# Layers 0 and 1 of a four-layer graph network: seven half products, both layers of a batch in turn, queues in program order

## The chip, the core and the metric

One core of a Trainium2 chip runs the whole kernel. The time is device microseconds of one execution; the median of three runs is compared. The engines are TensorE (PE, with its weight loads PEld), VectorE (DVE), ScalarE (ACT), GpSimd (POOL) and SyncE (SP), which here only issues DMAs.

## The reference

Sixteen graphs (batches) of 1024 nodes with 256 features, everything in float32, `adj` a dense 1024x1024 matrix per batch. Every layer is `x = x + layer(relu(layernorm(x)), adj)`:

```python
# layer 0: attention whose logits are e_n + f_m; e_n cancels in the quotient
h = hidden @ W_w.T + W_b
u = adj * exp(e[:, :, None] + f[:, None, :] + a_b);  a = u / sum(u, axis=2)
layer0 = a @ h
# layer 1: degree-normalised convolution
d = (sum(adj, -1) + 1e-5) ** -0.5
layer1 = (d[:, :, None] * adj * d[:, None, :]) @ (x @ weight) + bias
# layer 2: gated units over the nodes one after the other (a scan over 1024 nodes)
# layer 3: neighbour sums, then two products with an RMS norm between
```

So layers 0 and 1 each need, per batch, one sum over neighbours (`adj` times a 1024x256 matrix), a small product with a 256x256 matrix, and the weighted row sums of `adj`. Layer 2 visits the nodes in an order that is worked out on the chip from the zeros of `adj`.

## The kernel before

`layers_0_1` runs first, then `layer_2`, then `layer_3`. Only `layers_0_1` and the generator `orders` that runs inside it are touched by the change.

**A batch in layers 0 and 1.** `adjT` of a batch is loaded as two halves `at` of 512 columns (2 MB each), which stay for both layers; there are five such buffers. `prepare` takes the layer norm's statistics (L276, L277 on DVE, the power -0.5 in L83 on POOL), makes `q` and the attention weights `g`. `layer_0` computes the two weighted row sums (`pd`, L347, then `pn`, L357), then the sums over neighbours: `sums` has four parts, one for each half of the columns and each half of the 256 features, of eight 128x128 by 128x512 matmuls each (L295), copied from PSUM by ACT (L298) and DVE (L300). Then eight tiles are multiplied with `w0` (L365) and added to `x` by DVE (L366). `reshape` takes the statistics of the new `x` and ACT writes the normed `h1` (L287); `layer_1` does the same with `h1` and `w1` (L396, L397).

**The order of batches.** In step i, `layer_0(i)` comes first and `layer_1(i - 1)` after it, so that the norm between the two layers of a batch has products of another batch beside it. The parts of other work (`prepare`, `reshape`, jobs) are put between the four parts of the sums. No order is written out by hand: the framework's scheduler sets each engine's order, so that DVE's small instructions of several tasks are mixed.

**The order of the nodes.** `orders` returns two generators, which are advanced at such places. `places` reads diagonal blocks of `adj` in pieces of 16 rows (eight loads of 128 KB each, L99, prepared by L100) and assigns 128 nodes per block to sub-blocks: five small DVE instructions per node (L121 to L126), then ranks (L135, L137). `rest`, from step 9 on, makes index tables (L148, L163, L167), then the longest chains: two DVE instructions per node (L181, L182) on pieces loaded again, then maxima (L187 to L201), PE transposes (L208) and counters (L214 to L222), which become `more`, the register values that layer 2's loops read.

**The jobs.** `put_in_order(b)` is run from step 9 on, two batches a step: it loads diagonal blocks and rows (`ad`, `ab`, L409 to L413, and `h2`, L416), masks and scales them on POOL (L421 to L426), transposes `h2` and `ad` with the permutation `to` (L434, L447, L449) through `pt` in PSUM into the tile `hT`, multiplies `ab` with `h2` (L462), and stores the results for layer 2 with DMAs from POOL. The store of `hT` must end before the tile is written again.

**The start of layer 2** loads weights, `he` and `base`, POOL copies `hs` (L726), PE computes the gates' inputs (L735) and DVE adds the bias (L740).

## Time and profile before

| | |
|---|---|
| median of 3 runs | 4622.65 us (4618.07 to 4628.17) |
| span of the profiled execution | 4622.5 us, the only time that the page gives for it |
| mean granted TensorE clock | 0.978 |
| PE, DVE, POOL, ACT busy | 94%, 55%, 35%, 28% of the span |
| layers 0 and 1 on PE | to 1498.4 us |
| first PE, first DVE instruction of layer 2's gates (L735, L740) | 1511.25, 1520.0 us |

A group's line has the source line, the engine, the operation, the tile written and those read, the shapes, the count, then the busy time in us, the mean of one in ns, and the idle time of the engine before such instructions with what ended it. A float32 matmul shows as two records on PE, so 32 matmuls are "x64"; a transpose shows as one.

### The profile page before, as it was taken

The page shows a single profiled execution, that of the slowest core. Times are in us where ns is not written, and L with a number is a line of the kernel's source. Part 1 is how long each engine was busy: PE and PEld are TensorE (multiplying, and loading weights), DVE is VectorE, ACT ScalarE, POOL GpSimd, SP SyncE. Part 2 cuts the span into 40 slices and gives each one's busy share as a digit, 9 for nine tenths or more (in the row PEclk, how much of TensorE's full clock was granted, in tenths as well). Part 3 has the DMA queues.
Part 4 walks back from the last instruction along what each step waited for, and adds up shares of the span by engine and source line. Part 5 has one row for each costly group of instructions (what it writes and reads, how often), then busy time and mean ns, then how long its engine had stood idle before and what let it go on. Part 6 is the DMA issues. An engine that isn't in the chain of part 4 may idle for free. (4 is left out here: it accounts for less than half of the span.)

```text
span 4622.5 us, 54868 instructions
## 1 busy us (share of the span) xinstructions
PE 4336.9 (94%) x19223; PEld 2956.2 (64%) x19223; DVE 2535.5 (55%) x6436; ACT 1279.5 (28%) x2741; POOL 1623.5 (35%) x1914
## 2 busy tenths in 40 slices
PE   8999799999997899999999999999799999999998
PEld 4444345555554687778787878787655656565656
DVE  6667944555554344444444444445356666676765
ACT  1111111221121232323232323233234333333333
POOL 3222333433333333332332323234244444445352
PEclk9999899999998999999999999999899999999999
DMA  4333244455544644454444454542142222232310
GB/s 150 112 116 100 73 112 146 164 194 188 156 145 154 196 138 154 131 166 141 154 121 151 131 159 135 167 144 73 55 142 89 100 92 92 88 104 82 110 46 19
DMA packets 530989, 576.78 MB, mean 125 GB/s; under 512 B 42544, under 2 KB 439472, under 8 KB 528304
## 3 DMA queue, kind: packets, MB, share of 16 engines
q1 hardware_dynamic: 499536, 460.27, 32.0%
q0 software_dynamic: 31040, 111.44, 6.9%
q8 instruction: 206, 3.38, 0.3%
q14 instruction: 207, 1.70, 0.1%
HBM read 469.65 MB, written 116.65 MB: 127 GB/s over the span
## 5 line engine op out<-in xcount | busy, mean ns | idle before, releaser
L295 PE MATMUL pa<-at,h 128*128 128x512 f32 x1088 | 495.3, 608 | 33.0 <-DVE ag L300 33.0
L295 PE MATMUL pa<-at,q 128*128 128x512 f32 x960 | 423.6, 594 | 0.0
L623 PE MATMUL pf<-hb,ab 128*128 128x256 f32 x1568 | 407.9, 383 | 14.5 <-DMA hb<-hs_d 5.7
L295 PEld LDWEIGHTS pa<-at,h 128*128 128x128 f32 x1088 | 209.7, 196 | 277.6 <-issue 231.5
L735 PE MATMUL pf<-hs,wx 128*128 128x256 f32 x1536 | 348.9, 381 | 19.2 <-POOL hs L726 17.6
L735 PEld LDWEIGHTS pf<-hs,wx 128*128 128x128 f32 x1536 | 290.6, 191 | 62.5 <-POOL hs L726 19.4
L623 PEld LDWEIGHTS pf<-hb,ab 128*128 128x128 f32 x1568 | 280.3, 191 | 67.2 <-issue 14.2
L295 PEld LDWEIGHTS pa<-at,q 128*128 128x128 f32 x960 | 178.2, 190 | 215.9 <-issue 212.8
L1189 PE MATMUL ph<-bxt,hb 128*128 128x512 f32 x704 | 310.8, 597 | 3.8 <-ACT hb L1173 3.0
L1218 POOL TENSOR_TENSOR ss<-ss,sq 128x512 f32<-128x512 f32 x224 | 280.7, 1271 | 87.1 <-ACT sq L1216 83.4
L1023 POOL DMA_INDIRECT hs_d<-h,table x128 | 129.6, 1013 | 330.0 <-ACTq L1009 150.8
L1279 PEld LDWEIGHTS po<-w,hh 128*128 128x128 f32 x2048 | 235.9, 193 | 9.5 <-issue 7.2
L1279 PE MATMUL po<-w,hh 128*128 128x128 f32 x2048 | 240.1, 277 | 1.4 <-ACT hh L1262 0.7
L1189 PEld LDWEIGHTS ph<-bxt,hb 128*128 128x128 f32 x704 | 133.2, 192 | 164.7 <-issue 159.8
L740 DVE TENSOR_TENSOR gates<-pf,bias 128x512 f32<-128x512 f32 x128 | 88.3, 691 | 238.6 <-PE pf L735 238.6
L1261 DVE TENSOR_TENSOR hh<-hh,po 128x512 f32<-128x512 f32 x256 | 154.5, 681 | 96.7 <-PE po L1258 96.7
L83 POOL TENSOR_TENSOR rs<-rs_v,mhalf 128x8 f32<-128x8 f32 (+1 forms) x65 | 106.9, 1645 | 255.0 <-DVE rs_v L79 241.5
L771 PE MATMUL pf<-bd,h 128*128 128x384 f32 (+4 forms) x512 | 185.6, 454 | 5.3 <-ACT bs L610 2.8
L1216 ACT ACTIVATE sq<-hh 128x512 f32<-128x512 f32 x224 | 141.1, 630 | 164.3 <-DVE hh L1214 125.6
L830 ACT ACTIVATE r<-pr 128x256 f32<-128x256 f32 (+3 forms) x230 | 68.1, 348 | 403.5 <-PE pr L789 389.5
L1214 DVE SCALAR_TENSOR_TENSOR hh<-ph,b,u 128x512 f32<-128x512 f32 x192 | 144.0, 751 | 64.9 <-PE ph L1210 54.8
L774 DVE TENSOR_TENSOR bxt<-bxt,pf 128x384 f32<-128x384 f32 (+4 forms) x256 | 125.0, 501 | 97.0 <-PE pf L771 95.5
(296 smaller groups left out, 8473.1 us busy)
## 6 DMA issues: line engine op xcount, KB each, us to landing
at<-in_adjT SPq DMA_DIRECT2D x64, 1024.0 KB, 7.1
ab<-in_adj SPq DMA_DIRECT2D x128, 512.0 KB, 4.3
bxt<-in_adjT SPq DMA_DIRECT2D x88, 512.0 KB, 6.7
at<-in_adjT SPq DMA_DIRECT2D x40, 512.0 KB, 6.8
ad<-in_adj SPq DMA_DIRECT2D x128, 128.0 KB, 6.2
x_d<-x POOLq DMA_DIRECT2D x16, 1024.0 KB, 5.1
he_d<-h POOLq DMA_DIRECT2D x16, 1024.0 KB, 8.9
heT_d<-hT POOLq DMA_DIRECT2D x16, 1024.0 KB, 4.2
```

The lines of the kernel that those rows point to most:

```text
L295: nc.tensor.matmul(pa, h[:, mt, c * P : (c + 1) * P], at[n0 // 512][:, mt], start=mt == 0, stop=mt == NT - 1)
L623: nc.tensor.matmul(pb, ab[:, jts[k]], hb[:, jts[k]], start=k == 0, stop=k == len(jts) - 1)
L735: nc.tensor.matmul(pg[:, e], wx[:, c, q * D + e * P : q * D + (e + 1) * P], self.hs[:, c], start=c == 0, stop=c == DC - 1)
L771: nc.tensor.matmul(pf, h[:, g, c * P : (c + 1) * P], bd[:, g, b0 : b0 + n, S : S + far], start=True, stop=True)
L774: return lambda: nc.vector.tensor_add(to, to, pf)
L1023: nc.gpsimd.indirect_dma_start(out=hs_d[t][g][:, :], out_offset=row(1, g, t, s), in_=h[:, g], in_offset=None)
L1189: nc.tensor.matmul(pa, h[b][:, mt, c * P : (c + 1) * P], at[b][n0 // NH][:, mt], start=mt == 0, stop=mt == NT - 1)
L1214: nc.vector.scalar_tensor_tensor(hh[q][:, k], ph, b1[:, k : k + 1], u, op0=ALU.add, op1=ALU.add)
L1216: nc.scalar.activation(sq, hh[q][:, k], AF.Square)
L1218: nc.gpsimd.tensor_tensor(ss[q], ss[q], sq, ALU.add)
L1261: nc.vector.tensor_mul(hh[q][:, k], hh[q][:, k], pr)
L1279: nc.tensor.matmul(po[:, n], left[:, c, n * P : (n + 1) * P], right[:, c], start=onto is None and n == 0 and c == 0, stop=c == HH - 1, ski ...
```

## The change

The sums over neighbours are computed from halves in all three dimensions, with seven products of four matmuls in place of eight (`combos`, `sums`). The left factors are `q` or `h1`, combined by four DVE instructions per layer, two of them in place. The right factors are combinations of the quarters of `adjT` that are made once per batch and used in both layers: `t1` and `t3` by an accumulating DMA from POOL (`plus`), `t2` and `t4` by DVE (`add_halves`). One quarter is loaded twice. Ten quarter buffers (1 MB each) take the place of the five halves.

Both layers of a batch now run in turn in step i; only the product with `w1` and the addition to `x` of batch i - 1 are put off, to stand between layer 0 and layer 1 of batch i. The statistics of `x` for layer 0 and layer 2 move from DVE to ACT (`Moments`); the additions of `W_b` and `bias` on POOL work on two tiles at a time.

`manual_schedule` for all five queues: every engine runs its instructions in the order of the program. Other work is placed by hooks between the products. The two generators of `orders` become one, with a planned cost in us at each `yield`; `side(us)` advances it by about that much. Pieces are four rows (eight loads of 32 KB) in two buffers of their own, the next but one fetched when a piece is done. What is left of the generator at the end of the stage is run there. The jobs, two a step from step 9 on, run as a block after the `w1` product and after layer 1; the last two follow in step 16. Layers 2 and 3 are untouched.

The core of the diff (in the hooks, only the calls that the text speaks of):

```diff
-    def piece(j0, op, value):
-        nz = pool.tile([P, S, P], F32, name="ad")
-        for t in range(NT):
-            nc.sync.dma_start(nz[t * B : (t + 1) * B], a["adj"][:, t * P + j0 : t * P + j0 + S, t * P : (t + 1) * P])
-        nc.vector.tensor_scalar(nz[:, :, j0:], nz[:, :, j0:], 0.0, value, op0=op, op1=ALU.mult)
-        return nz
+    R = 4
+    pieces = deque()
+    def fetch(j0):
+        nz = pool.tile([P, R, P], F32, name="pc", bufs=2)
+        for t in range(NT):
+            nc.sync.dma_start(nz[t * B : (t + 1) * B], a["adj"][:, t * P + j0 : t * P + j0 + R, t * P : (t + 1) * P])
+        pieces.append(nz)
+    def piece(j0, op, value):
+        nz = pieces.popleft()
+        nc.vector.tensor_scalar(nz[:, :, j0:], nz[:, :, j0:], 0.0, value, op0=op, op1=ALU.mult)
+        return nz
...
+        fetch(0)
+        fetch(R)
+        yield 9.0
+        for j0 in range(0, P, R):
+            nz = piece(j0, ALU.is_equal, 2 * TOP)
...
+                if j < j0 + R - 1:
+                    yield 1.0
+            if j0 + 2 * R < P:
+                fetch(j0 + 2 * R)
+            yield 1.2
...
+    yield from places()
+    while not now["rest"]:
+        yield 99.0
+    yield from rest()
+now = {"rest": False}
...
+        ET = mybir.EngineType
+        st.enter_context(tc.manual_schedule(engines={ET.PE, ET.DVE, ET.Activation, ET.Pool, ET.SP}))
...
+        quarters = [big.tile([P, 4, 512], F32, name=f"at{k}") for k in range(10)]
+        Q = {b: {} for b in range(B)}
+        def get(b, name, m, n):
+            Q[b][name] = quarters.pop(0)
+            nc.sync.dma_start(Q[b][name], rows(a["adjT"][b])[:, 4 * m : 4 * m + 4, 512 * n : 512 * n + 512])
+        def drop(b, name):
+            quarters.append(Q[b][name])
+        def plus(b, name, other):
+            nc.gpsimd.dma_start(out=Q[b][name], in_=Q[b][other], accum_op=ALU.add)
...
+            def first(self, tiles):
+                junk = psum.tile([P, 512], F32, name="pt")[:, :D]
+                for t in tiles:
+                    nc.scalar.activation(junk, self.x[:, t], AF.Identity, accum_out=self.sum[:, t : t + 1])
...
-        def sums(at, h, ag):
-            def part(n0, c):
-                pa = psum.tile([P, 512], F32, name="pa")
-                for mt in range(NT):
-                    nc.tensor.matmul(pa, h[:, mt, c * P : (c + 1) * P], at[n0 // 512][:, mt],
-                                     start=mt == 0, stop=mt == NT - 1)
-                if c == 0:
-                    nc.scalar.copy(ag[:, c, n0 : n0 + 512], pa)
-                else:
-                    nc.vector.tensor_copy(ag[:, c, n0 : n0 + 512], pa)
-            return [lambda n0=n0, c=c: part(n0, c) for n0 in (0, 512) for c in range(DC)]
+        def combos(h):
+            a11, a12, a21, a22 = (h[:, m * 4 : m * 4 + 4, c * P : (c + 1) * P] for c in range(DC) for m in range(2))
+            s1, s2 = (big.tile([P, 4, P], F32, name=name) for name in ("s1", "s2"))
+            st = {"11": a11, "12": a12, "22": a22, "s1": s1, "s2": s2, "s3": a21, "s4": a12}
+            def first():
+                nc.vector.tensor_sub(s1, a21, a22)
+                nc.vector.tensor_sub(s2, s1, a11)
+            def second():
+                nc.vector.tensor_sub(a21, a11, a21)
+                nc.vector.tensor_add(a12, a12, s2)
+            return st, first, second
+        def sums(b, st, hooks, done=lambda name: None):
+            ag = big.tile([P, DC, N], F32, name="ag", bufs=2)
+            c11, c12, c21, c22 = (ag[:, c, n : n + 512] for c in range(DC) for n in (0, 512))
+            m = Q[b]
+            def product(left, right, pa, start=True):
+                for k in range(4):
+                    nc.tensor.matmul(pa, st[left][:, k], m[right][:, k], start=start and k == 0, stop=k == 3,
+                                     skip_group_check=True)
+                done(right)
+            bank = lambda: psum.tile([P, 512], F32, name="pa", bufs=4)
+            px = bank()
+            product("11", "b11", px)
+            nc.scalar.copy(c11, px)
+            hooks[0]()
+            py = bank()
+            product("12", "b21", py)
+            nc.vector.tensor_add(c11, c11, py)
+            hooks[1]()
+            product("s2", "t2", px, False)
+            nc.scalar.copy(c12, px)
+            hooks[2]()
+            pz = bank()
+            product("s1", "t1", pz)
+            hooks[3]()
+            product("s3", "t3", px, False)
+            nc.scalar.copy(c21, px)
+            nc.vector.tensor_sub(c22, pz, c21)
+            hooks[4]()
+            pw = bank()
+            product("22", "t4", pw)
+            nc.vector.tensor_add(c21, c21, pw)
+            hooks[5]()
+            product("s4", "b22", pz, False)
+            nc.vector.tensor_sub(c12, pz, c12)
+            hooks[6]()
+            return ag
+        def weights(x, ag, w, scale, then=lambda t: None):
+            for t0 in range(0, NT, 2):
+                po = psum.tile([P, 2, D], F32, name="pmm")
+                for t in (t0, t0 + 1):
+                    for c in range(DC):
+                        nc.tensor.matmul(po[:, t - t0], ag[:, c, t * P : (t + 1) * P], w[:, c],
+                                         start=c == 0, stop=c == DC - 1)
...
+                for t in (t0, t0 + 1):
+                    for c in range(DC):
+                        nc.tensor.matmul(po[:, t - t0], ag[:, c, t * P : (t + 1) * P], w[:, c],
+                                         start=c == 0, stop=c == DC - 1)
+                for t in (t0, t0 + 1):
+                    nc.vector.scalar_tensor_tensor(x[:, t], po[:, t - t0], scale[:, t : t + 1], x[:, t],
+                                                   op0=ALU.mult, op1=ALU.add)
+                    then(t)
...
+        def degrees(b):
+            m = Q[b]
...
+            for n0, (top, low) in ((0, ("b11", "b21")), (512, ("t3", "b22"))):
...
+            def run(self):
+                self.turn()
+                self.first()
+                self.order()
+                self.base()
+        def side(us):
+            left[0] += us
+            while left[0] > 0:
+                cost = next(math, None)
+                if cost is None:
+                    break
+                left[0] -= cost
+            left[0] = min(left[0], 0.0)
...
+        jobs = {i: (2 * (i - 9), 2 * (i - 9) + 1) for i in range(9, 16)}
+        jobs[16] = (14, 15)
...
+            def a1():
+                second()
+                add_halves(i, "t4", "t2", "b21")
+                late_norm(hi)
...
+                side(3.0)
+            def a3():
+                side(4.0)
...
+            def a4():
+                nonlocal_["rc"], nonlocal_["deg"] = over(i, ds)
...
+                side(1.5)
...
+                inverse(i, nonlocal_["deg"])
+                if run_a:
+                    run_a.scale()
+                side(2.0)
...
+                side(3.0)
...
+                    for name, mh, nh in (("b11", 0, 0), ("t1", 0, 1), ("b22", 1, 1)):
+                        get(i + 1, name, mh, nh)
+                ag = sums(i, left_of, [a0, a1, a2_, a3, a4, a5, a6])
+                mv = small.tile([P, NT, 2], F32, name="mv")
+                weights(x[i], ag, w0, nonlocal_["rc"], lambda t: stats(x[i], (t,), mv))
...
+                normed(h1[i], x[i], shift, rd, all_)
...
+                weights(x[i - 1], ags[i - 1], w1, dis[i - 1],
...
+                left_of, first, second = combos(h1[i])
+                first()
+                side(2.0)
+            if run_a:
+                run_a.run()
+                run_b.load()
...
+            def d0():
+                if ahead:
+                    plus(i + 1, "t1", "b11")
+                    get(i + 1, "t3", 0, 1)
+                plus_row(x[i], "bias")
+                if m2:
+                    m2.first(all_)
+            def d1():
+                second1()
+                if ahead:
+                    get(i + 1, "b21", 1, 0)
+                    begin_f(i + 1, all_)
+                if m2:
+                    m2.middle()
+                side(2.0)
...
+                    add_f(i + 1, hi)
+                    end_f(i + 1)
+                side(1.0)
...
+            def d5():
+                if ahead:
+                    Q[i + 1]["t2"] = quarters.pop(0)
+                    add_halves(i + 1, "t2", "t1", "b22")
...
+            ags[i] = sums(i, left_of, [d0, d1, d2, d3, d4, d5, d6], lambda name: drop(i, name))
+            if ahead:
+                ds = degrees(i + 1)
+                left_of, first, second = combos(q[i + 1])
+                first()
+                plus(i + 1, "t3", "b22")
+                plus_row(x[i + 1], "W_b")
+                Q[i + 1]["t4"] = quarters.pop(0)
+            if run_b:
+                run_b.run()
+            side(4.0)
+        for _ in math:
+            pass
```

## The prediction, made before the changed kernel ran

> **What bounds the kernel now.** I read the page's busy times first, then busy time by stretch, the groups and waits of the stretch in which layers 0 and 1 run, then the timeline of its ends.
>
> The page; then busy time by stretch (columns: stretch, length, then PE, PEld, DVE, ACT, POOL busy, granted clock, DMA share, GB/s):
> ```profile
> PE 4336.9 (94%) x19223; PEld 2956.2 (64%) x19223; DVE 2535.5 (55%) x6436; ACT 1279.5 (28%) x2741; POOL 1623.5 (35%) x1914
> ```
> ```profile
> 66.65:789.46 722.81, 662.76 (x2068) 340.03 (x2066) 477.37 (x1802) 129.48 (x268) 206.71 (x203) 0.96 0.34 103
> 789.46:1355.05 565.59, 534.13 (x1967) 302.68 (x1965) 302.21 (x905) 118.48 (x240) 213.00 (x228) 0.99 0.54 176
> 1355.05:1498.40 143.35, 120.05 (x437) 73.95 (x435) 67.65 (x257) 24.03 (x46) 47.16 (x48) 0.89 0.39 128
> ```
> PE is the bound: 92% busy in the first stretch (batches before the jobs that put rows in order), 94% in the second (two jobs a batch). DMA is at half or less, ACT at a fifth. The degree products start at 53.08, 94.22 ... 789.46 ... 1355.05: 81.8 us a batch over the first nine, 94.3 over the six with jobs.
>
> The groups (busy, mean ns, then idle before):
> ```profile
> L295 PE MATMUL pa<-at,h 128*128 128x512 f32 x1088 | 495.3, 608 | 33.0 <-DVE ag L300 33.0
> L295 PE MATMUL pa<-at,q 128*128 128x512 f32 x960 | 423.6, 594 | 0.0
> L83 POOL TENSOR_TENSOR rs<-rs_v,mhalf 128x8 f32<-128x8 f32 x48 | 80.1, 1668 | 126.7 <-DVE rs_v L79 113.3 <-DVE mv L277 12.3
> L181 DVE SCALAR_TENSOR_TENSOR ad<-o_sub,ad 128x127 f32<-128x127 f32 (+63 forms) x127 | 37.6, 301 | 0.2
> L182 DVE SCALAR_TENSOR_TENSOR o_bins<-ad,o_bins 128x127 f32<-128x127 f32 (+63 forms) x127 | 37.1, 292 | 0.2
> ```
> The neighbour sums are 919 us of PE. L181/L182 are the chain rows that the old order hid under them.
>
> The PE timeline (start, length, bracket: idle before it):
> ```profile
> 66.65 27.73 PE L295 MATMUL pa<-at,h 128*128 128x512 f32 x64
> 127.39 9.79 PE L295 MATMUL pa<-at,h 128*128 128x512 f32 x16 [3.71 <-DVE ag L300]
> 918.32 7.13 PE L295 MATMUL pa<-at,h 128*128 128x512 f32 x16 [2.25 <-DVE ag L300]
> 1010.11 8.76 PE L295 MATMUL pa<-at,h 128*128 128x512 f32 x16 [2.27 <-DVE ag L300]
> ...
> 1497.94 0.44 PE L468 MATMUL pt<-to,bo 128*128 128x128 f32 x2 [0.57 <-ACT bo L464]
> 1511.25 1.22 PE L735 MATMUL pf<-hs,wx 128*128 128x256 f32 x2 [12.87 <-POOL hs L726]
> ```
> 64 records are 32 matmuls, so one costs 0.866 us. Sixteen records should take 6.93; after waits of 3.71, 2.25 and 2.27 they take 9.79, 7.13 and 8.76. A gap costs itself and up to 2.9 more. Layers 0 and 1 end at 1498.4, and 12.87 of wait follows.
>
> **Products removed.** 28 matmuls for 32, in 2 layers of 16 batches: 128 x 0.866 = 110.8 us off PE. PE work of a batch becomes 2 x 24.2 (sums) + 1.8 (L357) + 2 x 7.0 (L365, L396) + 3.6 (L347) = 67.8 us; a job adds 8.5 (its transposes and L462).
>
> **Cover removed.** Before, layer 1 of the previous batch (28 us) lay between layer 0 of a batch and its own layer 1. Now only the 7.0 us of w1 products do. I count from the start of layer 0's products.
>
> A batch in which `places` runs beside: the seven products and L357 end at 26.1. DVE, from 7.1 on (second product), has evictions 4 x 0.69, combinations 2 x 0.69, t4 2 x 1.38, small rows 1.7 and 10.5 planned units of `side`. One node of `places` is planned at 1.0-1.2, but its five rows (253+165+250+206+308 ns) in strict order, with 0.04 after each dependent one, take about 1.25: 10.5 units are 13.3 us. Together 22, so the last eviction ends at 29.1, and `side(3.0)`, 3.8 us, at 33. Behind it on DVE stand the additions to x, and PE, having filled both pmm buffers at 29.5, waits until 34.5: 5 us. An addition with its statistics is 0.48+0.41+0.17 = 1.06 in order, eight take 8.5: 41.5. Then rs_v, the power on POOL (1.67), rd and shift with hops: 44. The w1 additions are queued on DVE behind rd, so PE waits another 2.5; layer 1 starts at 48.8, where PE's own work is 40. Layer 1 and degrees take 24.2 + 3.6 + 1.5 (the third bank's subtraction is late behind eight 0.86 us steps of `add_f`). With 2 us of slow clock: 80 a batch.
>
> The Trainium skill's page TensorE: Matmul & The Clock Gate ("Why this matters for your kernels") advises against PE gaps over about 3 us, since the clock then halves, for a window of about 3.4 us. By the page the 5 us gap would cost 1.7 and the 2.5 us gap nothing, 2.4 us less over eight batches than my 2.0 each; but 2.27 us of gap cost 1.8 in the row above, and I keep the row.
>
> Without `side` the last eviction ends at 27, layer 1 starts at 43.7; a job run in strict order, on two pt buffers and one hT, takes 10.5. A batch with two jobs: 43.7 + 24.2 + 1 + 3.6 + 21 = 93.5.
>
> **Moved to ACT, POOL and DMA.** 256 tile statistics leave DVE (256 x 0.58 = 149 us); 512 activations of the L287 kind (0.589) come to ACT, 302 us in 1500, hidden by an engine 20% busy; uncovered, 19 us a batch. POOL's additions get wider and no more. SP's `t3` load stands behind a piece load that waits for DVE; it still lands 14 us before the degrees. A fifth quarter (1 MB) per batch and two accumulating 1 MB DMAs hide in the idle half of the DMA; uncovered, a quarter at 176 GB/s is 6 us a batch. No row shows an accumulating DMA: below, a plain POOL-queued 1 MB copy (heT_d 4.2 us, he_d 8.9), above, three times the slower, 27. `t3` has 13.9 us from the degrees to its product. I take 10, near the nearest row (he_d), so hidden.
>
> **Sum of the stretch.** Start 30 (before: 24.3; v and the statistics now stand ahead in order), batch 0 74, seven at 80, batch 8 76 (`places` ends in it), four at 93.5, two at 97 (`side` again), batch 15 90, the last two jobs one after the other 41: 1439. Before: 1498.4. Gain 59, not 110.
>
> **The tail that appears.** `side` spends 22.5 units a batch. `places` needs 188.7, so it ends in batch 8, before the flag is set; the generator then yields 99, and `side` must repay it: `rest` starts in batch 12. In the changed program's order, all 32 pieces of the chain stand on DVE behind the last job's last copy, and PE has the transposes of `top` ahead of layer 2's first product. Nothing covers it. DVE's part: 127 x 0.50 (L181 to L182 dependent) + 32 x 0.35 (the L100 kind) = 75. But a piece has two buffers, and its eight loads go out one by one. The nearest rows, SP's issues with the time to landing:
> ```profile
> L409 SPq DMA_DIRECT2D ad<-in_adjT x16: 340/346/352, 501.1 to 1468.3; - x16
> DMA to landing us min/median/max: 1.8/1.9/1.9
> ...
> L99 SPq DMA_DIRECT2D ad<-in_adj x128: 312/447/2387, 24.9 to 1417.2; - x128
> DMA to landing us min/median/max: 3.7/6.2/9.7
> ```
> L409 is 64 KB, L99 128 KB; a new load is 32 KB, nearer to L409: 8 x 0.4 + 1.9 = 5.1 after a buffer is freed, so (5.1+2.4)/2 = 3.75 a piece, 120 us. With L99's landing (3.2+6.2+2.4)/2 = 5.9: 188; with free loads 75. Then L187 to L222 without cover, 20: 140 (95 to 208).
>
> The Trainium skill's page DMA: Bandwidth & Descriptors ("Rules for kernel authors") says that under 64 KB one pays mostly overhead, and to coalesce; if a 32 KB load is no cheaper than L99's 128 KB, the tail is 208.
>
> Layer 2 and 3 have the same instructions in the same order but for SP's. Before, DVE's first gates row stood at 1520.0; after, 1439 + 140 + 2 = 1581. That is +61, on a span of 4622.5, which equals the median of the runs (4622.65): **4684**.
>
> **Rivals.** *Faster: PE stays fed.* My walk puts 164 us of stalls in the stretch, 10 a batch. For: the same rows overlap better if `side` runs as planned. Against: DVE is in strict order and the two waits are structural. With none, the stretch is 1275 and the time 4520; at 5 a batch 4598. It decides below 6 a batch. *The accumulating DMA is slow.* At 20 us instead of 10, PE waits 6 in 15 batches, +90: 4774; at 27, 4879. *Pieces land as L99's do:* +68, 4752. That fewer products are run is not in doubt: the order has 28 matmuls for each sum.
>
> **Chances.** What a measurement of this kernel can tell from no change is 0.2%, 9 us. Forecast 0.54 (own range 4635 to 4740); PE fed 0.18; slow accumulation 0.11; slow pieces 0.13; stalls of 6 to 7 a batch, no change, 0.04. So faster 0.18, same 0.04, slower 0.78. Range 4570 to 4790: it takes in most of the faster case and both slower ones at their middle prices.
>
> **What would show it.** Right: the sums at about 804 us for 919; a stretch of 110 to 150 us before layer 2 with PE idle, DVE in chain rows and waits for the piece's load; waits of 2 to 5 us in the w0 and w1 products on DVE's x; batches of 80 and 93. Wrong: batches under 75 (the walk), waits for an at buffer ahead of the fifth product (the accumulation), a tail under 100 (the piece load).

## The result and the profile after

The changed kernel takes 4804.99 us (median of 4 runs, 4802.45 to 4805.32), the kernel before in the same session 4622.88 us: a ratio of 1.0392, 95% interval 1.0377 to 1.0407. The forecast was 4684: the sign was right, the loss three times as large. The profiled execution spans 4803.4 us.

The page's busy times; then busy time by stretch, columns as before (the last row lies between the last job and DVE's first gates row):
```profile
PE 4277.7 (89%) x18967; PEld 2933.2 (61%) x18967; DVE 2735.1 (57%) x6213; ACT 1608.4 (33%) x3861; POOL 1610.1 (34%) x1816
```
```profile
45.73:771.90 726.17, 639.82 (x1986) 327.61 (x1985) 549.93 (x1492) 313.68 (x897) 180.91 (x143) 0.95 0.47 141
771.90:1387.59 615.69, 540.40 (x1933) 311.49 (x1932) 364.54 (x843) 252.04 (x690) 230.22 (x205) 0.94 0.57 189
1387.59:1524.70 137.11, 94.68 (x381) 63.50 (x379) 50.80 (x116) 34.08 (x80) 54.92 (x47) 0.86 0.46 132
1524.70:1697.03 172.33, 11.53 (x33) 6.47 (x34) 93.11 (x376) 0.84 (x2) 5.64 (x8) 0.51 0.32 81
```
PE has 88% in the first two rows (92 and 94% before), 69% in the third (84%), and then 161 us with next to nothing to do. The last job ends at 1524.7 (before: 1498.4), so the stretch did not get shorter by 59 us, it got 26 longer; and 172 us pass from there to the first gates row.

The groups of the sums, and PE's longest waits (total, times, longest):
```profile
L378 PE MATMUL pa<-at,q 128*128 128x512 f32 x640 | 301.6, 622 | 41.3 <-DVE ag L398 41.2
L378 PE MATMUL pa<-at,h 128*128 128x512 f32 x640 | 287.5, 603 | 11.7 <-DVE ag L398 5.9
L378 PE MATMUL pa<-at,s 128*128 128x512 f32 x512 | 224.9, 592 | 0.0
```
```profile
PE pt L232 <- DVE o_top L209: 135.4, 7, 133.9
PE pmm L414 <- DVE x L417: 55.8, 27, 4.5
PE pa L378 <- DVE ag L398: 47.1, 14, 9.5
PE pt L523 <- DVE hT L528: 45.2, 7, 16.9
```
The sums are 814 us of PE in place of 919: the products are gone. What PE does now is wait: 134 us in one piece for the chain of `rest`, 56 for the additions to `x`, 47 for the fourth quarter `c22` (L398), 45 for DVE's copies into the jobs' buffer `hT` (L528).

Lengths read from the traces (us). A batch runs from one row of the degree products to the next (L464, which stands some 16 us inside a batch of the forecast's walk: so its 90 and 41 us at the end are 115 here); "last" goes from batch 15's row to the end of the last job, "tail" from there to the last write of `more` (L250), "start" from that to DVE's first gates row.

| kernel | batches 1-6 | 7-8 | 9-12 | 13-14 | last | tail | start |
|---|---|---|---|---|---|---|---|
| the forecast | 480 | 156 | 374 | 194 | 115 | 140 | 2 |
| changed | 506 | 145 | 399 | 216 | 137 | 153 | 19 |
| e1_rest_at_once | 506 | 150 | 437 | 249 | 138 | 19 | 20 |
| e2_moments_later | 499 | 147 | 398 | 210 | 136 | 154 | 19 |
| e8_three_pieces | 455 | 145 | 400 | 218 | 138 | 137 | 19 |
| e10_x_first | 500 | 145 | 399 | 212 | 136 | 153 | 20 |
| e9_hT_halves | 510 | 145 | 393 | 209 | 132 | 153 | 19 |
| e16_side_later | 524 | 146 | 399 | 208 | 138 | 153 | 20 |
| e4_eight_products | 499 | 157 | 411 | 201 | 141 | 154 | 19 |
| e13_eight_on_e8 | 471 | 156 | 411 | 201 | 142 | 137 | 20 |
| e11_scheduler | 479 | 174 | 434 | 200 | 110 | 9 | 20 |
| e12_best_in_order | 455 | 150 | 437 | 228 | 126 | 19 | 19 |
| e20_best_own_pool | 464 | 150 | 437 | 222 | 119 | 23 | 4 |

### The profile page after: what moved, and what is told of

Read it like the earlier page. It is cut to its first block, busy times and chain, and to the rows that moved or that the text cites. A ratio compares the mean times of both kernels' runs of the same rounds, so it can differ in the third digit from the quotient of the medians.

```text
span 4803.4 us, 56185 instructions
## 1 busy us (share of the span) xinstructions
PE 4277.7 (89%) x18967; PEld 2933.2 (61%) x18967; DVE 2735.1 (57%) x6213; ACT 1608.4 (33%) x3861; POOL 1610.1 (34%) x1816
## 5 line engine op out<-in xcount | busy, mean ns | idle before, releaser
L378 PE MATMUL pa<-at,q 128*128 128x512 f32 x640 | 301.6, 622 | 41.3 <-DVE ag L398 41.2
L414 PE MATMUL pmm<-w,ag 128*128 128x256 f32 x1024 | 265.3, 413 | 59.9 <-DVE x L417 55.8
L378 PE MATMUL pa<-at,h 128*128 128x512 f32 x640 | 287.5, 603 | 11.7 <-DVE ag L398 5.9
L414 PEld LDWEIGHTS pmm<-w,ag 128*128 128x128 f32 x1024 | 204.3, 205 | 124.8 <-DVE x L417 88.4
L378 PEld LDWEIGHTS pa<-at,q 128*128 128x128 f32 x640 | 124.2, 200 | 199.2 <-issue 149.3
L378 PE MATMUL pa<-at,s 128*128 128x512 f32 x512 | 224.9, 592 | 0.0
L378 PEld LDWEIGHTS pa<-at,h 128*128 128x128 f32 x640 | 122.5, 194 | 164.0 <-issue 138.0
```

The lines of the kernel that those rows point to most:

```text
L378: nc.tensor.matmul(pa, st[left][:, k], m[right][:, k], start=start and k == 0, stop=k == 3, skip_group_check=True)
L414: nc.tensor.matmul(po[:, t - t0], ag[:, c, t * P : (t + 1) * P], w[:, c], start=c == 0, stop=c == DC - 1)
```

## The experiments

All ratios are to the kernel before, timed in the same call, with 95% intervals.

### The tail

**e1_rest_at_once**
```diff
-        while not now["rest"]:
-            yield 99.0
```


> The debt of 99 in the generator of orders is taken out: `rest` follows `places` at once, from batch 7 on, in the hooks. Theory A (the tail is that debt): the 153 us between the last job and the end of `more` fall to under 40 us, and what `rest` costs DVE (some 170 us of work in seven batches with slack) lengthens batches 7 to 15 by 10 to 40 us in all, so 4700 to 4740 us against 4805. Rival (a queue in strict order has no free place for this work): batches 7 to 15 grow by about what the tail loses, 90 us or more, and the time stays within 30 us of 4805.

4748.04 us, 1.0261 (1.0239 to 1.0283). The tail falls from 153 to 19 us, as theory A has it; but batches 9 to 14 grow by 70, nearly twice what it allowed. Both sides have half of it: the debt makes the tail, and the strict order charges half of it again where the work goes. In those batches DVE waits 45 us for pieces and PE 43 for `c22`, a wait that the changed kernel has almost only in batches 1 to 6: what `places` does to batches 1 to 6, `rest` does to the later ones.

**e3_pieces_two_queues**
```diff
-                nc.sync.dma_start(nz[...], a["adj"][...])
+                eng = nc.scalar if both and t % 2 else nc.sync      # both: in the chain of rest only
+                eng.dma_start(nz[...], a["adj"][...])
```


> In the chain of `rest` every other one of a piece's eight loads is issued from ACT's queue in place of SP's. Theory C (a piece takes 4.1 us because SP issues its eight loads at 0.52 us each): the piece falls to about 3 us, where DVE's eight operations or the landing bound it, and the time by 25 to 40 us, to 4765 to 4780. Rival, the prediction's sum (eight issues and a landing of 1.9 us in a row, so that a landing bounds with two buffers): half the issue time goes as well but the pitch stays above 3.7 us, and the time falls by under 14 us.

4779.73 us, 1.0335 (1.0310 to 1.0359), 25 under the changed kernel. The 32 pieces of the chain come 3.57 us apart on average, in the changed kernel 4.23. So the issues count, though the pitch did not come down to 3.

**e19_own_pool**
```diff
+            own_pool = st.enter_context(tc.tile_pool(name="orders01", bufs=1))
-            math = orders(big, psum)
+            math = orders(own_pool, psum)
```


> The tiles of `orders` lie in a pool of their own behind the others, so that the memory which layer 2's first tiles take over is given up by the last job and not by the last DVE operation of `rest`. The prediction had layer 2's first loads in flight during the tail; in the changed kernel they are issued 0.4 us behind `more` and the first gates come 19.4 us behind it. Theory I (the pool's release alone keeps the loads back): first gates 2 to 6 us behind `more`, 13 to 17 us faster than 4805. Rival (they wait for DMAs or queues of the tail as well): first gates stay 17 us or more behind `more`, the time within 8 us.

4783.15 us, 1.0355 (1.0340 to 1.0370): 22 less, more than expected; the first gates come 16 us earlier, the rest of the gain lies behind them. The wait of SP's queue at the end of the changed kernel, then the issues in this one, and this one's DVE timeline:
```profile
SPq L816 <- DVE more L250: 23.1, 1, 23.1
```
```profile
1529.52 125.35 SPq L102 DMA_DIRECT2D pc<-in_adj  x240
1655.29 0.38 SPq L817 DMA_DIRECT2D wx<-in_W_iouxT  x1
```
```profile
1681.31 0.67 DVE L1001 TENSOR_TENSOR gates<-pf,bias 128x512 f32<-128x512 f32 x1
1681.91 0.66 DVE L249 TENSOR_SCALAR o_left<-o_need 1x8 f32<-1x8 f32 x8
1682.61 0.18 DVE L250 CAST more<-o_left 1x64 int32<-1x64 f32 x1
```
The weights' load goes out with the last piece, 27 us ahead of `more`, and the first gates row now stands even before `more`. Theory I holds: the pool's memory held layer 2 back, for DVE instructions whose results its loads do not need. The first line of the second fence also has the pace of SP: 240 issues in 125.35 us, 0.52 each, 4.2 us for a piece of eight, with its waits for a freed buffer in it.

### The batches beside `places`

The trace of the changed kernel in batch 3 shows what is late. ACT, DVE, PE and SP timelines:
```profile
300.43 0.39 ACT L333 ACTIVATE pt<-x 128x256 f32<-128x256 f32 x1 [17.58 <-DMA x<-in_x]
```
```profile
303.06 0.69 DVE L398 TENSOR_TENSOR ag<-pa,ag 128x512 f32<-128x512 f32 x1 [10.31 <-ACT ag L397]
```
```profile
303.81 5.12 PE L378 MATMUL pa<-at,q 128*128 128x512 f32 x8 [9.49 <-DVE ag L398]
```
```profile
257.86 27.07 SPq L102 DMA_DIRECT2D pc<-in_adj  x16
285.04 2.34 SPq L293 DMA_DIRECT2D at<-in_adjT  x3
287.54 1.03 SPq L278 DMA_DIRECT2D x<-in_x  x1
```
Read upwards: SP issues the pieces one by one as DVE frees their buffers; then three quarters; then the next `x`, which lands 13 us later. ACT, in program order, stands before that `x` for 17.58 us with the copy of `c21` (L397) behind it; DVE waits for the copy 10.31, PE for DVE 9.49, and PE's eight records then take 5.12 where 3.60 is usual. Together 11 us, most of the 12 to 15 that batch 3 (86 us) has over batches without pieces (71 to 74).

**e2_moments_later**
```diff
 def a3():
-    mean[i + 1] = Moments(x[i + 1])
-    mean[i + 1].first(lo)
 def a4():
-    mean[i + 1].first(hi)
+    mean[i + 1] = Moments(x[i + 1])
+    mean[i + 1].first(all_)
```


> ACT's first half of the sums of the next x moves from the hook ahead of the copy of c21 to the hook after it; nothing else is touched. Theory B (batches 1 to 6 take 84 us because the next x lands some 13 us late behind the pieces of `places` on SP's queue, ACT stands before it with the copy of c21 queued behind, and so DVE's c22 and PE's seventh product are late): PE's wait for c22, 47 us in all, falls to under 10 us, batches 1 to 6 fall from 84 to 75-78 us, and the time to 4745 to 4775 us. Rival, the prediction's own cause (DVE's work of the `side` hooks is what is late): batches 1 to 6 stay within 2 us of 84 and the time within 12 us of 4805.

4795.69 us, 1.0361 (1.0339 to 1.0383): a miss for theory B. What its rival expected came (83 us a batch, 9 us in all), but the prediction's own cause is not thereby shown. The wait for `c22` falls from 47 to 20 us, but that for the additions rises from 56 to 72. DVE's timeline, in batches 3 and 2:
```profile
301.12 0.17 DVE L336 TENSOR_SCALAR m_neg<-m_sum 128x8 f32<-128x8 f32 x1 [9.31 <-ACT pt L333]
```
```profile
211.29 0.34 DVE L107 TENSOR_SCALAR pc<-pc 128x352 f32<-128x352 f32 x1 [7.96 <-DMA pc<-in_adj]
```
`x` and the pieces are as late as before, and the next instruction in line that needs it (or a late piece) holds the next queue. Moving the reader does not help while the load is late.

**e8_three_pieces**
```diff
-            nz = pool.tile([P, R, P], F32, name="pc", bufs=2)
+            nz = pool.tile([P, R, P], F32, name="pc", bufs=3)
```
(and two 64-byte tiles of `orders` in `junk`, to make room.)

> Three buffers for the pieces of adj in place of two, with the fetch still two pieces ahead, so that the buffer which a fetch on SP's queue asks for was given up one piece earlier. Theory D (in batches 1 to 6 SP stands with a piece's fetch until DVE has worked off a piece, 147 us in four batches of e2_moments_later, and the quarters and the x queued behind it on SP come late; everything that needs x then stalls, on whichever strict queue it stands): SP's wait for DVE falls to under a third, batches 1 to 6 from 84 to 74-78 us, the time to 4740 to 4770. Rival E (x is late because three quarters of 1 MB lie ahead of it in the queues of the DMAs): batches stay over 82 us and the time within 15 us of 4805.

4736.35 us, 1.0256 (1.0231 to 1.0281), 69 under the changed kernel and better than expected. Batches 1 to 6 take 76 us each. SP's waits in the changed kernel between 204 and 545 us, then here:
```profile
SPq L102 <- DVE o_bins L135: 90.8, 11, 25.9
SPq L102 <- DVE pc L107: 67.2, 7, 17.4
```
```profile
SPq L102 <- DVE pc L107: 5.1, 3, 2.2
SPq L102 <- DVE o_bins L135: 4.6, 3, 1.7
```
Theory D holds: a fetch that waited for its buffer kept everything behind it on SP. In batches 1 to 6 PE's wait for `c22` falls from 46 us to 5, and PE is busy 422 us in place of 435 with the same matmuls, at a granted clock of 0.98 for 0.94. The tail gains 16 as well: with the buffer free in time a piece takes 3.72 us there, for 4.23. SP's timeline in this tail, and the landing of its loads:
```profile
1480.99 109.95 SPq L102 DMA_DIRECT2D pc<-in_adj  x232
```
```profile
DMA to landing us min/median/max: 2.4/2.4/3.7
```
Without waits for a buffer an issue takes 0.47 us, and eight of them are about what a piece takes here. Of the 4.2 us a piece in the changed kernel, about 0.5 is the wait for the buffer.

**e10_x_first**
```diff
-        for name, mh, nh in (...): get(i + 1, name, mh, nh)     # at the start of the batch
 def a2_():
     load_x(i + 1)
+    for name, mh, nh in (...): get(i + 1, name, mh, nh)
```


> The loads of the next batch's first three quarters are issued after the load of the next x in place of before it; the pieces' fetches stay where they are. Rival E of the run before: x lands some 4 us after its issue in place of 13 to 14, ACT's and DVE's waits behind it go, batches 1 to 6 fall to 74-78 us, the time to 4740 to 4770. Theory D (SP is held by the pieces' buffers): a gain of 1 to 5 us a batch at the most, the time 4775 to 4800. Both: if the quarters then come too late for the transposed sum of degrees or the accumulating DMA, batches 7 and 8, which are at 74 and 71 us, grow.

4791.94 us, 1.0375 (1.0351 to 1.0399); 7 us in batches 1 to 6, and not the 40 to 60 of rival E, which falls. ACT's waits for `x` do go down there, from 89 us to 36, but DVE's waits for pieces go up from 16 to 37: the pieces are as late as before, and the stall is theirs now.

### What the seven products are worth

**e4_eight_products**
```diff
-    st = {"11": a11, "12": a12, "22": a22, "s1": s1, "s2": s2, "s3": a21, "s4": a12}
+    return {"11": a11, "12": a12, "21": a21, "22": a22}, nothing_, nothing_
...
+    for (l1, r1), (l2, r2), to, last in ((("11", "b11"), ("12", "b21"), c11, False), (("21", "b11"), ("22", "b21"), c21, True),
+                                       (("11", "t3"), ("12", "b22"), c12, False), (("21", "t3"), ("22", "b22"), c22, True)):
```


> The seven products alone are undone: each layer's sums are eight products of raw quarters, without the combinations of adj or of x; the order of the batch, the hooks, the fetches, the jobs and the strict queues stay (the four quarters of the next batch are all loaded at the start of a batch). Theory A (the 128 products taken out are worth their 0.866 us each on PE, 110.8 us, and the loss comes from elsewhere): 60 to 111 us slower than the changed kernel, 4865 to 4916. Rival (the combinations cost DVE and ACT as much as PE saves, so the seven products are worth nothing in this order): within 20 us of 4805, or faster.

4815.46 us, 1.0411 (1.0387 to 1.0435): no difference from the changed kernel that these intervals tell apart. The rival has it. (With the products go the combinations, the accumulating DMAs and one load a batch.) Batches 1 to 6, the changed kernel's row and this one's:
```profile
120.22:626.61 506.39, 435.23 (x1345) 223.22 (x1344) 392.23 (x1120) 220.48 (x637) 121.71 (x96) 0.94 0.47 143
```
```profile
124.70:623.47 498.77, 465.05 (x1442) 242.01 (x1441) 292.78 (x1022) 212.84 (x621) 109.65 (x84) 0.97 0.31 103
```
PE has 30 us less to do with seven products and idles 37 more; DVE is busy 99 us longer, of which some 34 are not the combinations' own work but instructions that stand while POOL adds (below, under the jobs). In batches 7 and 8, which load no pieces, the seven are worth 12 us (145 against 157).

**e13_eight_on_e8**: the same edit in e8_three_pieces.

> e8_three_pieces with eight products of raw quarters in place of the seven. What the 128 products are worth where PE waits less: if batches 1 to 8 are then bound by PE, eight products cost 4 to 7 us a batch there and 50 to 90 us in all (4785 to 4825 against 4736). Rival (even so DVE and the strict order set the pace, and the seven are worth as little as in e4_eight_products, 10 us): 4735 to 4755.

4766.90 us, 1.0316 (1.0299 to 1.0333), 31 above e8_three_pieces, between the two cases. Of PE's 35 us less in batches 1 to 6, 16 come through; in batches 13 and 14, where DVE also makes the index tables of `rest`, eight products are 17 faster: PE is busy as long with seven as with eight there (187 and 186 us, at a granted clock of 0.91 and 0.99).

### The jobs and the `side` work

**e9_hT_halves**
```diff
-                    hT = big.tile([P, DC, N], F32, name="hT")
                     for c in range(DC):
+                        hT = big.tile([P, N], F32, name="hT", bufs=2)
...
+                        nc.gpsimd.dma_start(heT_d[b][:, c], hT)
...
-                    ao = big.tile([P, NT, 2 * P], F32, name="hT")
+                            ao = big.tile([P, h, 2 * P], F32, name="hT", bufs=2)    # h = NT // 2, each half stored when full
```


> The one 8 KB buffer that a job's transposed states and then its reordered adjacency go through is split into two of 4 KB, each stored as soon as its half is there; six DMA issues a job on POOL in place of four. Theory F (the job's waits for that buffer's stores, DVE 48 us and PE 45 us in batches 9 to 16, are on the path): batches 9 to 15 and the last two jobs lose 25 to 60 us together, the time 4745 to 4780. Rival (a store's landing time is what is waited for, whatever its size, and POOL's two more issues come on top): within 12 us of 4805.

4788.13 us, 1.0362 (1.0338 to 1.0387). Batches 9 to 14 and the last stretch lose 20 us, less than expected. DVE's wait for the states' store falls from 48 us to 17, so theory F has a wait that lies on the path; but PE's wait for DVE's copies into `hT` (L523), 45 us, is still 45: those copies are late in DVE's own order, and not by the buffer.

What stands ahead of them there can be read in the changed kernel's trace. DVE, POOL and PE timelines at the start of batch 11's second job:
```profile
1040.08 5.81 DVE L363 TENSOR_TENSOR s<-s,q 128x512 f32<-128x512 f32 x1
1045.81 0.68 DVE L528 COPY hT<-pt 128x512 f32<-128x512 f32 x1
```
```profile
1040.11 5.22 POOL L353 TENSOR_TENSOR x<-x,W_b_sb 128x512 f32<-128x512 f32 x4
```
```profile
1046.55 1.11 PE L523 MATMUL pt<-to,h 128*128 128x128 f32 x4 [4.59 <-DVE hT L528]
1047.45 5.28 PE L535 MATMUL pt<-h,ab 128*128 128x256 f32 x16
```
L363, a combination for the next batch, is the instruction ahead of the job's first copy. It lasts 0.69 us as a rule; here it lasts 5.81, as long as POOL's four additions of `W_b`. PE waits 4.59 for the copy, and its next row takes 5.28 in place of 3.69. The same happens in each of batches 9 to 14: 28 us of this wait and 10 of slower matmuls behind it. With eight products, which have no combination in that place, the wait is 1 us (e4 and e13). In the whole stretch 22 of POOL's 32 blocks of four additions have one DVE instruction beside them that is 3.6 to 6.0 us longer than the median of its line; beside the narrower additions of the kernel before there is one of over 3 us. No run moved or narrowed the additions alone.

**e16_side_later**
```diff
 def a5(): ...
-    side(2.0)
 def a6(): ...
-    side(3.0)
 def d0(): ...
+    side(2.0)
 def d4(): ...
+    side(3.0)
```


> The changed kernel with one thing moved: the 5 units of `side` work that stand ahead of layer 0's weight products (hooks a5 and a6) go into layer 1's sums (hooks d0 and d4). Theory H (PE's 56 us of waits for the first evictions of the weight products come from that `side` work, as the prediction had it with 5 us a batch): those waits fall under 25 us, and as the pieces still hold SP in batches 1 to 6 only part of it shows: 15 to 40 us faster than 4805. Rival (there the evictions wait in DVE's order for something else, and the `side` work is late wherever it stands): within 12 us of 4805.

4808.14 us, 1.0403 (1.0387 to 1.0418): no gain. Batches 13 and 14 lose 8 us and batches 1 to 6 get 17 more. PE's waits before the last job (in the changed kernel 55.8 us for the additions and 47.1 for `c22`, shown above):
```profile
PE pa L378 <- DVE ag L398: 72.5, 18, 10.2
PE pmm L414 <- DVE x L417: 31.9, 18, 2.3
```
The wait goes where it was expected to go, and comes back as a wait for `c22`. Theory H has the place right and the price wrong.

### The order

**e11_scheduler**
```diff
-            st.enter_context(tc.manual_schedule(engines={ET.PE, ET.DVE, ET.Activation, ET.Pool, ET.SP}))
```


> The order of layers 0 and 1 on the queues is not the program's any more: the scheduler orders the same instructions on all five engines by its own estimates, as it does for the kernel before; work and buffers are unchanged. Theory G (strict order in all queues is what turns each late transfer into a stall of PE, and what puts all of the debt behind the last job): the sums and jobs run closer together, 40 to 150 us faster than 4805, and `rest` still cannot start before its place in the program, or starts early. Rival (the order written by hand is better than the scheduler's for this program): slower than 4805 by 20 us or more.

4659.12 us, 1.0084 (1.0056 to 1.0112), 146 faster. But the table shows where: the last job ends at 1524.1, as in program order (1524.7). All of the gain is the tail, 9 us for 153: the scheduler sets the chain among the jobs although the program has it behind them. Against e1, which has the chain ahead of the last job in program order and ends that job at 1600.4, its order is 76 us shorter.

**e14_scheduler_pieces** (three piece buffers and halves of `hT` in e11_scheduler)

> e11_scheduler (the scheduler's order) with three piece buffers and the jobs' buffer in halves. If the two waits hold in its order as well: 20 to 70 us under 4659, that is 4590 to 4640, which may beat the kernel before (4617 to 4623). Rival (the scheduler already works around them): within 12 us of 4659.

**e15_scheduler_rest** (the same without the debt)

> The run before and without the debt of 99, so that the chain of `rest` stands earlier in the program that the scheduler is given. The tail of e11_scheduler was 10 us already, so theory A (the tail was the debt alone in strict order) expects within 15 us of e14_scheduler_pieces; a gain of 10 to 30 us if the chain's pieces, spread over more batches, no longer disturb the last ones.

4697.90 us, 1.0159 (1.0140 to 1.0178), and 4696.80 us, 1.0160 (1.0143 to 1.0177). The first is a miss: what helps in program order costs 39 us here, PE's wait for `c22` going from 59 to 80. Other buffers give the scheduler another order on every engine; which part of it is to blame was not tried. The second run's expectation holds.

### Towards a better version

**e12_best_in_order**: e1, e8, e9 together, and in the last step
```diff
-                    run_a.mask()
-                    run_a.scale()
 ...
                         nc.vector.scalar_tensor_tensor(m2.shift, mv2[:, :, 0], -1.0, m2.rs, op0=ALU.mult, op1=ALU.mult)
+                        run_a.mask()
+                        run_a.scale()
```


> Program order kept on all queues, with the causes found so far taken out together: three piece buffers, no debt of 99, the jobs' buffer in halves, and in the last batch the last but one job's masks and scalings behind the norm's root on POOL. If the causes add (69 us of e8_three_pieces, 17 of e9_hT_halves, 57 of e1_rest_at_once or more, as the pieces no longer hold SP in batches 9 to 15, some 10 of the last batch): 4620 to 4655 us, level with the kernel before or up to 0.8% above. If `rest` in the hooks costs the job batches as much without the pieces' wait as with it: 4650 or more. Under 4610 only if job batches with `rest` come down to 100 us.

4653.89 us, 1.0072 (1.0056 to 1.0089), at the upper end. The causes add, but `rest` still costs batches 9 to 14 about 64 us against the chain left to the end (e9: 601, here 665).

**e17_best_side_later**: e12 with e16's move.

> e12_best_in_order with the same move. In that kernel the job batches with `rest` take 105 to 118 us against 99 without, and PE waits 46 us for the evictions of the weight products after batch 8. Theory H: those waits halve, a late PE no longer runs cold behind them, and the time falls by 20 to 45 us, to 4610 to 4635, level with the kernel before (about 4621). Rival: within 12 us of 4654.

4653.31 us, 1.0068 (1.0054 to 1.0082): nothing, as in e16. In batches 9 to 14 and behind, the wait for additions falls from 46 to 18 us, that for `hT` rises from 29 to 43.

**e18_best_side_more**: e17 with `side(2.5)` in d0, `side(1.0)` in d2, `side(3.5)` in d4.

> The run before with 2 more units of `side` work a batch, in layer 1's sums (hooks d0, d2, d4), so that `rest` is done before the last job and the tail of 20 us goes. If DVE has room there: 10 to 20 us faster than e17_best_side_later, which would beat the kernel before. Rival: the sums grow by what the tail loses, within 8 us of it.

4681.26 us, 1.0129 (1.0114 to 1.0145), 28 slower than e17: a miss. The tail does go (`more` is written 90 us before the last job ends), but batches 9 to 14 take 39 us more: PE's wait for `c22` behind batch 8 is 49 us, 16 in e17.

**e20_best_own_pool**: e17 with e19's pool.

> e17_best_side_later with the same pool. Theory I: the tail there is 19 us from the last job to `more` and 20 us from there to the first gates; the second part falls to 2 to 8 us: 4635 to 4643, still 0.3 to 0.5% above the kernel before. Rival as in the run before: within 8 us of 4653.

4640.52 us, 1.0039 (1.0027 to 1.0051). As expected, and the best of the versions: 165 us under the changed kernel, still slower than the kernel before.

**e21_side_in_jobs**
```diff
                     self.first()
+                    side(4.0)
                     self.order()
 ...
-                    side(4.0)
+                    if not run_a:
+                        side(4.0)          # hook a3
```


> e20_best_own_pool with the `side` work of the job batches put where DVE stands idle: 4 units inside each job, between the states' turn and the adjacency's order (DVE waits there some 4.5 us for PE), in place of the 4 units of hook a3, ahead of c22. If these gaps are free: `rest` is done before the last job, the tail of 23 us from the last job to `more` falls to under 5 us, the batches 9 to 14 lose 1 to 3 us each: 4600 to 4625 us, which would beat the kernel before (about 4620) or draw with it. Rival (the work makes the jobs' evictions late, as 2 more units a batch made the sums late in e18_best_side_more): 4640 or more.

4678.99 us, 1.0124 (1.0104 to 1.0144): a miss. `rest` is done 60 us before the last job ends, and batches 9 and 10 fall to 103 and 102 us, both as hoped, but from 11 on they take 116 to 131. ACT's waits there:
```profile
ACT pt L332 <- DMA x<-in_x: 74.2, 4, 20.3
```
`x` is late again (29 us of this wait in e20). On SP, fetches of pieces wait 98 us for DVE in these batches, now also with three buffers, and a job's load 126 us for the buffer `ad`, and `x` stands behind both: the same mechanism.

## Why the prediction missed

The forecast's own points, against the table (its sum reached the first gates at 1581; they stood at 1697.0).

- **Products removed.** Right on PE: the sums fell by 105 us (forecast 110.8). As time, they are worth 12 us in batches 7 and 8, nothing measurable in the whole changed kernel (e4), and 31 us with three piece buffers (e13).
- **The walk of a batch beside `places`: 80, measured 84.4 (+26 us over six).** This is the step that failed first. It took the last eviction to be late by DVE's `side` work, and priced waits of 5 and 2.5 us in the weight products. They are 2.45 and 1.93 in batch 3; the large wait is the one it did not have, 4.9 to 9.5 us for `c22`. The prediction followed one load, `t3`, past the pieces on SP's queue, and did not follow the one issued next to it, the next `x`, to ACT, which the change had just given its statistics; nor did it have a wait of DVE for the pieces themselves. e8 shows the cause, 51 us in these batches. They then take 76 us each, so 80 was no walk of what happens there: without the late loads it was too slow.
- **Batches 7 and 8: 156, measured 145.** The walk was too slow here as well: 74 and 71 us. `places` ended in batch 8 as planned (at 703 us), but its last piece was worked off in batch 6, and the ranks that are left for batch 7 cost less than nodes.
- **Job batches 93.5, 97 and the last stretch: 683 in all, measured 753 (+70).** "A job run in strict order takes 10.5" is the mis-sized term. In batches 9 to 14 (+48) the first job of a batch takes 11.2 to 13.2 us on PE and the second 15.7 to 18.1, 43 us more than 10.5 each. The stores of `hT` are 20 of the 70 (e9). A larger term was put at nothing: "POOL's additions get wider and no more". The second job's wait behind these additions, 28 us, and the slower matmuls after it, 10, are read from the trace (under e9), not taken out by a run. The job batches' sum also had no term for PE's clock, where the `places` batches had 2 us; PE is busy 540 us in them for 509 counted, at a granted clock of 0.95 and 0.93, and some 2 of the 5 us a batch are work that was counted too low (69.7 for 67.8 in batches 7 and 8, at 0.99). In the last stretch (+22) e9's stores are 5, and the norm's root behind a job's masks on POOL about 6 (e12's 126 against e9's 132; the other two parts of e12 alone leave it at 138). The rest is open, and a wait that is moved comes back elsewhere (e16, e17).
- **The tail: 140, measured 153.** The mechanism was right (e1): the chain stands behind the last job, and the piece's load bounds it. Two terms of the piece were mis-sized: an issue, 0.4 us by the duration of its row, is 0.47 from start to start, and a landing, 1.9 by L409, is 2.4 (both in e8). With them the prediction's own formula gives (8 x 0.47 + 2.4 + 2.4) / 2 = 4.28 us a piece; 4.23 was measured. The last 20 us, from L209 to L250, were as put down. The Trainium skill's page DMA: Bandwidth & Descriptors ("Rules for kernel authors") has transfers under 64 KB pay mostly overhead; a landing of 2.4 us for 32 KB beside 1.9 for 64 KB fits that. What the runs do not show is the prediction's reading of it, that a small load then costs as much as L99's, for which it had a tail of 208.
- **Layer 2's start: 2, measured 19.** The prediction let its loads run in the tail. They waited for the memory of the pool, that is for `more` (e19). The trace of before had shown 21.6 us between the last job and the gates, and nothing in the change took them away.

Together 26 - 11 + 70 + 13 + 17 = 115 of the 116 us between 1581 and 1697. Of the rivals, "PE stays fed" is out, "pieces land as L99's do" also, and so is the slow accumulating DMA:
```profile
at<-at POOLq DMA_DIRECT2D x30, 1024.0 KB, 6.9
```
6.9 us to landing, under the 10 that the forecast took, and no wait of PE names it. The range ended at 4790 because its upper end came from those two; no room was left for a wait that the walk did not have. That the sign was right says little for the sum: one stretch of it was 11 us too long, and the others 126 too short.

## What to carry to other kernels

In a strict order a queue is one line: before a load is placed behind a DMA that waits for a buffer, follow every load behind it to its reader, and what stands behind that reader on its engine; one more buffer for the small load was worth more here (69 us) than an eighth of the products. A stall moves when its reader is moved; it goes only when its source is on time. And less work on the busiest engine is worth only what its neighbours leave: at best 31 us of 111 came through here, while DVE was busy 99 us longer in six batches and PE's clock fell behind its waits; what share each had was not separated. A wider instruction on an engine with time to spare is not free either: look at what the other engines' rows do beside it.

## What the runs showed of the hardware

- SP issued 32 KB loads every 0.47 us where no buffer was waited for (232 in 109.95, e8), more than the 0.42 that the median row of one lasts, and every 0.52 with two buffers (240 in 125.35, e19). Alternating them with ACT's queue brought the distance of two pieces from 4.23 to 3.57 us, a third buffer alone to 3.72.
- An accumulating DMA of 1 MB between two tiles landed in 6.9 us, between the plain 1 MB stores of the same run, 4.2 (`heT_d`) and 8.5 (`he_d`).
- PE behind a gap of 9.49 us took 5.12 us for 3.60 us of matmuls, 1.5 lost. A longer gap did not cost more: in batches 1 to 6 six gaps of 4.85 to 9.49 us lost 1.5 to 2.9, the shortest the most:
```profile
130.45 6.46 PE L378 MATMUL pa<-at,q 128*128 128x512 f32 x8 [4.85 <-DVE ag L398]
```
  The Trainium skill's page TensorE: Matmul & The Clock Gate ("What's actually happening") would give 1.7, an estimate from its window of 3.4 us at half clock. Two of the six gaps are near it (1.5 and 1.7); four lost 2.6 to 2.9, and there the measurement decides.
- While POOL ran its four additions of 128x512, 5.2 to 5.3 us, DVE often stood in one instruction for about as long: L363 lasted 5.81 us for its usual 0.69, and 22 blocks of 32 have such a row.
